# Attention stage of a two-layer kernel: pools and loads that run on across images, an image that begins within its own split, separate buffers for the two halves' planes, and a product held back

## The chip, the cores and the metric

The kernel runs on one core of a Trainium2 chip. A core has a matrix engine (TensorE; PE in the profile, its weight loads PEld), a vector engine (VectorE, DVE), a scalar engine (ScalarE, ACT), GpSimd (POOL) and SyncE (SP), whose queue issues most of the DMAs here.[...] The metric is the device time of one execution in microseconds (us), lower is better.

## The reference

`x` is 4 images of 96 channels, 128x128 pixels, float32. Two layers follow each other, each added to its input after a group norm.

```python
# layer 0: a state space block on 192 inner channels
z = silu(depthwise3x3(in_w @ gn(x)));  four scans over z (rows, columns, both ways)
x = x + out_w @ layernorm_c(y0 + y1 + y2 + y3)
# layer 1
xr, x1, x2 = relu_split_norm(gn(x))            # positive part and negative part, each normed over the image
key, qry  = conv3x3(x1, aw1), conv3x3(x2, aw2) # cut into 3x3 patches
attn      = softmax(key . qry / sqrt(C*9))     # gives a 96x96x3x3 kernel of each image
y1        = norm(conv3x3(conv3x3(x1, aw3), attn))
y2        = norm(conv3x3(x2, w_conv2)) * x1
x = x + xr + w_full @ concat(y1, y2) + b_full
```

What matters here is layer 1: the softmax needs the whole image, and only then can the last convolution (with weights made from it) begin. The split norm needs two passes over the image: sums first, then the two halves.

## The kernel before

The program is written with a tile framework: the code emits instructions in an order that is their priority, a planner orders them for each engine by that priority, by dependencies and by its own cost estimates, and a tile whose slot is still held waits for its release. Pools that are closed and opened again reuse the same memory, so the first tiles of the new pool wait for the last uses of the old one.

Two streams are interleaved by `co_run(left, light, pace)`: after each step of `left` (with a cost), steps of `light` worth `pace` times this cost are emitted. `Later` holds follow-up work (evacuations, stores) for a few ticks.

For each image b the light stream holds, in this order: `norm` (`ssm_output`: the output projection of layer 0), `split` (`split_norm`), both for the image ahead, and `close` (`attn_output`: the last 1x1 convolution and residual) of the image behind. The left stream is the attention:

- Image 0 is worked by `direct_maps`: direct 3x3 convolutions in strips of 6 rows. As it goes, `lift` turns the value map `vd` into planes `vp` (4 rows a step, 32 steps, twelve DVE instructions each, L1426 to L1435). At its end stand the remaining lifts, then `taps.weights()`: softmax, nine transposes (L1696), `products_weights` on DVE (L1258 to L1264), a store to `watd`. Its last convolution is in `attention`, which loads `watd` again (`wa`).
- Images 1 to 3 are worked by `attention` wholly. Convolutions are done over planes: each row of pixels is turned into six planes (`planes_of`), so that a 3x3 convolution takes six products for four columns. Strips are 12 rows, 11 to an image. For each strip there are two maps m (0: key and value from x1, 1: query and w_conv2 from x2); each has a first `products` of 128 output rows and a second one of 64. Their results leave PSUM through ACT copies `ends` and `odd` (L1540) and DVE sums (L1554 to L1562). `PairTaps` collects key times query. After the last strip `weights()` makes `wa`, and 11 strips m=2 of the last convolution follow, from `vp` to `od`.

`split_norm`'s second pass goes through 16 pieces of 8 rows. ACT writes the scaled input to PSUM (L1219), DVE masks it into a tile `half` (L1223; one buffer for each side, `half0` and `half1`), and `planes_of` makes six planes and stores them (L1442) in `x1p` or `x2p`. For x1 that is done by two ACT multiplications into `x4` and `x2` (L1393, L1394) and ten POOL instructions (L1401 to L1406, and L1371 four times); for x2 wholly by nine DVE instructions (`at_once`, L1376 to L1383, L1371 four times). Both go through one buffer `diff`, and share the two buffers `pl`. `value_out` does the same as the x1 form for the value map, two halves of a strip, with 128 partitions and one buffer each of `x4`, `x2`, `diff`, `pl`.

`attention` opens its pools `d1` and `d2` anew for each image, loads its first two strips (`ya`, `yc`) once they are open, and flushes its `Later` at the end. Between two images the light stream is drained.

The image loop before:

```python
light = chain(*([] if b else [light]), *after)
left = imgs[b].attend(psl)
co_run(left, light, 1.0 if b else 1.5)
drain(left)
drain(light)
```

Of the kernel before, what the change touches and what calls it, by code (L numbers as in the profile page):

```python
# [9 lines left out]
F32 = mybir.dt.float32  # L10
# [58 lines left out]
def kernel(  # L69
# [992 lines left out]
    def split_norm(xnew, x1d, x2d, stats, keep, cnt, ps, side, planes, vector):  # L1062


        with ExitStack() as pools:
# [120 lines left out]
            def stored(i, m, h):  # L1186
                if planes:
                    return planes_of(
                        later, p2, h, RS, lambda pl: store_planes(nc.sync, m, i * RS, RS, pl),
                        vector=vector(i, m is x2d),  # L1190
                    )
                at = (i * RS + 1) * PW
                return lambda: nc.scalar.dma_start(m[:, at : at + RS * PW], h)

            half = [p2.tile([C, RS * PP], F32, name=f"half{j}", bufs=1) for j in range(2)] if planes else []
            for h in half:
                nc.gpsimd.memset(h.rearrange("p (a b) -> p a b", b=PB)[:, :, TN:PB], 0.0)
            for i in range(NS):
                y = ahead.pop(0)
                piece(i + 3)  # L1200
                for side_, m in ((0, x1d), (1, x2d)):
                    op = ALU.is_le if side_ else ALU.is_gt
                    if planes:
                        h = half[side_]
# [143 lines left out]
    def planes_of(later, pool, t, r, then, most=RS, vector=False, bufs=2, p=C):  # L1348
# [6 lines left out]
        def made():  # L1355
            f = pool.tile([p, most, 6 * TN + 4], F32, name="diff", bufs=1)[:, :r]
            pl = pool.tile([p, NP, most * TN], F32, name="pl", bufs=bufs)[:, :, : r * TN]
            at, out = 0, []
            for n in (2 * PB, 2 * TN, 2 * PB):
                out.append(f[:, :, at : at + n])  # L1360
                at += n
            return out, pl

        def sums(eng, mid, outer, pl):
            f1, f2 = mid[:, :, 0:TN], mid[:, :, PB : PB + TN]
            f3, f0 = outer[:, :, 0:TN], outer[:, :, TN:]
            for i, op, x, y in (
# [3 lines left out]
                op(pl[:, i].rearrange("p (h t) -> p h t", t=TN), x, y)  # L1371

        def at_once():
            (mid, outer, df), pl = made()
# [7 lines left out]
            for i, f in ((3, AA), (4, -AA)):  # L1382
                stt(  # L1383
                    pl[:, i].rearrange("p (h t) -> p h t", t=TN),
                    df[:, :, 0:TN], f, df[:, :, PB : PB + TN], ALU.mult, ALU.add,
                )
            sums(nc.vector, mid, outer, pl)
# [9 lines left out]
        def differences(x4, x2):  # L1397
            (mid, outer, df), pl = made()
            d1, d2 = df[:, :, 0:TN], df[:, :, PB : PB + TN]
            sub, add = nc.gpsimd.tensor_sub, nc.gpsimd.tensor_add  # L1400
            sub(mid, v[:, :, 2 * PB :], x4[:, :, : 2 * PB])  # L1401
            sub(outer, v[:, :, 1 : 1 + 2 * TN], x4[:, :, 2 * PB : 2 * PB + 2 * TN])
            sub(d2, v[:, :, 3 * PB : 3 * PB + TN], v[:, :, PB : PB + TN])
            sub(d1, x2[:, :, 1, 0:TN], x2[:, :, 0, 0:TN])
            for i, op in ((3, add), (4, sub)):
                op(pl[:, i].rearrange("p (h t) -> p h t", t=TN), d2, d1)  # L1406
            sums(nc.gpsimd, mid, outer, pl)
# [174 lines left out]
    class Taps:  # L1582
# [90 lines left out]
        def weights(self):  # L1673


            self.later.flush()
# [13 lines left out]
            yield from self.rest  # L1690
# [10 lines left out]
            self.wt = wt  # L1701
            self.later.flush()
# [139 lines left out]
    def attention(img, ps):  # L1842


        with (
            tc.tile_pool(name="d1", bufs=1, side="left") as p1,
            tc.tile_pool(name="d2", bufs=2, side="left") as p2,
        ):
            later = Later()
            chunks = strips_of(AR // 2)  # L1850
            chunks = [(c[0][0], sum(r for _, r in c)) for c in chunks]
            todo = [(2, c) for c in chunks]
            if not img.mapped:
                todo = [(m, c) for c in chunks for m in (0, 1)] + todo
            maps = (img.x1p, img.x2p, img.vp)
            raw, cols = {}, {}

            def load(c, k):

                if c >= len(todo):  # L1860
                    return
                m, (r0, r) = todo[c]
# [572 lines left out]
```

## Time and profile before

| | |
|---|---|
| runs | 6845.72 us median of 3 (6822.49 to 6851.2) |
| profiled execution | 6817.06 us; its span, first to last instruction, 6815.3 us |
| mean granted TensorE clock | 0.874 of full speed |
| PE busy over the span | 5528.0 us (81%) |
| DVE busy | 4821.4 us (71%) |
| ACT busy | 3807.2 us (56%) |
| POOL busy | 3411.4 us (50%) |
| image 0's last convolution | about 3755 to 3904 us |
| image 1 | about 3990 to 4942 us |
| image 2 | about 4991 to 5942 us |
| image 3 and the end | about 5990 to 6815 us |

A share of busy time is an average over stages with different limits; the change touches only what lies behind about 3300 us. The granted clock falls to half when PE stands still, so a stall also makes the first matmuls behind it slower.

### The profile page before, as it was taken

What the parts mean: (1) busy time and instruction counts of PE and PEld (TensorE: products, weight loads), DVE (VectorE), ACT (ScalarE), POOL (GpSimd) and SP (SyncE); (2) the same over time, 40 slices, a digit from 0 to 9 for tenths busy, and PEclk for the clock granted to TensorE, in tenths of its full rate; (3) what the DMA queues carried; (4) which work ended last, traced back from release to release, by engine and by line L of the source; (5) the groups of instructions that cost most, each with busy time, mean ns of one, the idle gap of its engine ahead of it and who ended that gap; (6) DMA issues with size and microseconds to landing.
All of it is one profiled execution on the core that took longest, in us unless ns stands there. A gap on an engine that the chain in (4) does not pass through costs nothing. (4 is left out here: it accounts for less than half of the span.)

```text
span 6815.3 us, 76516 instructions
## 1 busy us (share of the span) xinstructions
PE 5528.0 (81%) x23256; PEld 2349.2 (34%) x23256; DVE 4821.4 (71%) x7737; ACT 3807.2 (56%) x4751; POOL 3411.4 (50%) x2680
## 2 busy tenths in 40 slices
PE   5889978878886519999994759876889876889986
PEld 2333323322221104444332223444333444335652
DVE  3257779989896578889547844677855676987567
ACT  1257768777875476676324534654544654544552
POOL 2236759879795439889322344466024565034410
PEclk9999989989996659999996878887989877989997
DMA  7666777866766666756656755544865555865454
GB/s 168 167 163 179 199 211 201 232 168 179 217 177 171 173 199 195 218 171 183 186 158 163 210 148 158 144 126 132 231 160 160 143 132 134 223 174 148 111 147 144
DMA packets 882103, 1176.28 MB, mean 173 GB/s; under 512 B 215230, under 2 KB 740102, under 8 KB 869212
## 3 DMA queue, kind: packets, MB, share of 16 engines
q1 hardware_dynamic: 858076, 1116.43, 60.7%
q0 software_dynamic: 16208, 38.42, 2.1%
q10 hardware_dynamic: 7408, 16.53, 0.8%
q8 instruction: 187, 3.06, 0.2%
q14 instruction: 224, 1.84, 0.1%
HBM read 766.61 MB, written 334.57 MB: 162 GB/s over the span
## 5 line engine op out<-in xcount | busy, mean ns | idle before, releaser
L621 PE MATMUL bank<-y,wp 128*128 128x512 f32 (+3 forms) x3584 | 1313.3, 624 | 86.4 <-DMA y<-y 34.7
L854 POOL TENSOR_TENSOR y<-y,dl 128x1024 f32<-128x1024 f32 x384 | 1055.1, 2748 | 268.1 <-DVE dl L846 234.9
L821 POOL TENSOR_TENSOR dl<-dl,u 128x1024 f32<-128x1024 f32 x384 | 1007.2, 2623 | 219.3 <-ACT dA L797 111.7
L842 DVE TENSOR_TENSOR_SCAN dA<-dA,pBC 128x512 f32<-128x512 f32 x768 | 981.7, 1278 | 30.8
L1469 PE MATMUL two<-ya,wd 128*64 128x192 f32 (+3 forms) x2376 | 597.3, 433 | 267.1 <-DMA ya<-x1p 91.7
L735 PE MATMUL pBC<-xr,wbc 60*128 60x512 bf16 (+1 forms) x1536 | 457.2, 403 | 329.0 <-DVE dA L842 257.7
L621 PEld LDWEIGHTS bank<-y,wp 128*128 128x128 f32 (+3 forms) x3584 | 457.7, 169 | 755.2 <-issue 656.9
L2075 PE MATMUL bank<-y,wn 128*128 128x384 f32 (+5 forms) x2408 | 685.0, 509 | 39.5 <-DMA y<-x2d 18.5
L1894 ACT COPY yb<-ya 64x768 f32<-64x768 f32 (+1 forms) x660 | 538.1, 815 | 316.1 <-PE two L1469 151.9
L846 DVE TENSOR_TENSOR dl<-dA,pBC 128x512 f32<-128x512 f32 x768 | 528.8, 689 | 259.8 <-PE pBC L735 186.1
L664 ACT ACTIVATE dl<-pd,dtb 128x512 f32<-128x512 f32 x768 | 485.6, 684 | 181.5 <-PE pd L735 167.2
L1469 PE MATMUL two<-yb,wd 128*64 128x192 f32 (+3 forms) x2376 | 568.9, 415 | 0.0
L825 DVE TENSOR_TENSOR pBC<-dl,pBC 128x512 f32<-128x512 f32 x768 | 527.2, 686 | 11.7 <-POOL dl L821 10.8
L1955 POOL COPY own<-ring 32x512 f32<-32x512 f32 (+1 forms) x198 | 214.9, 1120 | 514.9 <-DVE ring L1562 463.9
L1005 PE MATMUL bank<-y,outws 96*96 96x512 f32 x512 | 446.4, 1010 | 0.7 <-ACT st L961 0.7
L1469 PEld LDWEIGHTS two<-ya,wd 128*64 128x64 f32 (+1 forms) x2376 | 266.5, 174 | 522.2 <-issue 234.7
L2075 PEld LDWEIGHTS bank<-y,wn 128*128 128x128 f32 (+3 forms) x2408 | 313.0, 170 | 358.9 <-issue 200.7
L797 ACT ACTIVATE dA<-dl,negA 128x1024 f32<-128x1024 f32 x384 | 420.3, 1142 | 2.3
L664 ACT ACT_TABLE_LOAD x245 | 314.3, 1283 | 96.2 <-PE pd L735 89.1
L735 PEld LDWEIGHTS <-wbc 60*128 60x128 bf16 (+1 forms) x1536 | 103.4, 96 | 765.2 <-issue 751.6
L1469 PEld LDWEIGHTS two<-yb,wd 128*64 128x64 f32 (+1 forms) x2376 | 295.9, 175 | 144.7 <-issue 35.3
L1469 PE MATMUL two<-ya,wa 128*96 128x384 f32 (+1 forms) x528 | 226.5, 512 | 130.9 <-DMA wa<-watd 78.9
(307 smaller groups left out, 9546.6 us busy)
## 6 DMA issues: line engine op xcount, KB each, us to landing
u<-zb SPq DMA_DIRECT2D x192, 1024.0 KB
yms<-y SPq DMA_DIRECT2D x96, 512.0 KB
y<-yms SPq DMA_DIRECT2D x64, 768.0 KB
xn<-xnew SPq DMA_DIRECT2D x128, 384.0 KB
ya<-vp SPq DMA_DIRECT2D x120, 336.0 KB
y<-y SPq DMA_DIRECT2D x128, 258.2 KB
zb<-z SPq DMA_DIRECT2D x64, 512.0 KB
ya<-x1p SPq DMA_DIRECT2D x90, 336.0 KB
```

What stands on the lines that cost most here:

```text
L621: nc.tensor.matmul(blocks(pz[p:e]), lhsT=ws[k][:, d, c : c + e - p], rhs=window(ys[k], at, d, n), start=(i == 0), stop=(i == len(terms) - 1),)
L664: nc.scalar.activation(dst, src, AF.Softplus, bias=bias)
L735: nc.tensor.matmul(p, lhsT=w[rows], rhs=xr[rows, at : at + CH], start=True, stop=True)
L821: nc.gpsimd.tensor_mul(t, t, u_view(n))
L825: nc.vector.tensor_mul(p, live[n]["dl"][:, bass.ts(half, CH)], p)
L842: nc.vector.tensor_tensor_scan(h, h, p, init, ALU.mult, ALU.add)
L846: nc.vector.tensor_mul(live[n]["dl"][:, sl], live[n]["dA"][:, sl], live[n]["C", half])
L854: nc.gpsimd.tensor_add(v, v, t.rearrange("p (a b) -> p a b", b=W))
L1005: nc.tensor.matmul(to, lhsT=outws[:, j], rhs=rhs, start=(j == 0), stop=(j == 1))
L1469: nc.tensor.matmul(of(to[p:e], r), lhsT=w[:, i, c : c + e - p], rhs=tiles(t[k][PAIR[i]][:, SLOT[i]], o, r), start=(k == 0), stop=False,)
L1894: nc.scalar.copy(yb[k][64 * h - 64 : 64 * h, :, :n], ya[k][0:64, :, h * TN : h * TN + n])
L2075: nc.tensor.matmul(pc[p:e, :n].rearrange("p (h w) -> p h w", w=W), lhsT=w[:, c : c + e - p], rhs=v[:, :, 0:W], start=(i == 0), stop=(i == ...
```

## The change

What it does, part by part:

1. Attention's pools `d1` and `d2`, its `Later` and its list of strips become one object `Attention` for all images. The list runs on from image to image, so the first two strips of an image are loaded two strips before the image ahead of it ends. `later` is no longer flushed at an image's end; `close` ticks it until that image's last result is stored (`finished`).
2. `drain(light)` after each image goes; only ahead of images 2 and 3 is the light stream drained. So image 1 begins while its own split is still under way; a load calls `until`, which emits as many steps of the split as its rows need.
3. In `split_norm` `half0` has two buffers, the DVE form has its own planes `plv` and `diff`, and the POOL form has `pl` (one buffer) and works in place: the differences overwrite `x4` and `x2`, one goes through plane 4. The number of instructions is the same.
4. The last second product of map 1 is held back: a third of it goes ahead of the last key times query sums, two steps behind the softmax, the rest behind the making of `wa`. In `direct_maps` the held product goes ahead of those sums.
5. In `direct_maps` the remaining lifts go behind `weights()` and the store of `watd`; the pool `lifts` moves into its pools.

The core of the diff:

```diff
 def split_norm(..., done):
+                    def then(pl):
+                        store_planes(nc.sync, m, i * RS, RS, pl)
+                        done[m is x2d] = (i + 1) * RS
-            half = [p2.tile([C, RS * PP], F32, name=f"half{j}", bufs=1) for j in range(2)] if planes else []
+            half = [
+                [p2.tile([C, RS * PP], F32, name=f"half{j}{k}", bufs=1) for k in range(2 - j)]
+                for j in range(2)
...
-                        h = half[side_]
+                        h = half[side_][i % len(half[side_])]
 def planes_of(...):
         def at_once():
-            (mid, outer, df), pl = made()
+            f = pool.tile([p, most, 6 * TN + 4], F32, name="diff", bufs=1)[:, :r]
+            mid, outer, df = f[:, :, : 2 * PB], f[:, :, 2 * PB : 130], f[:, :, 130:]
+            pl, to = planes("plv", 1)
...
         def differences(x4, x2):
-            (mid, outer, df), pl = made()
-            d1, d2 = df[:, :, 0:TN], df[:, :, PB : PB + TN]
+            mid, outer = x4[:, :, : 2 * PB], x4[:, :, 2 * PB : 2 * PB + 2 * TN]
+            d1 = x2[:, :, 0, 0:TN]
+            pl, to = planes("pl", 1)
-            sub(mid, v[:, :, 2 * PB :], x4[:, :, : 2 * PB])
-            sub(outer, v[:, :, 1 : 1 + 2 * TN], x4[:, :, 2 * PB : 2 * PB + 2 * TN])
-            sub(d2, v[:, :, 3 * PB : 3 * PB + TN], v[:, :, PB : PB + TN])
-            sub(d1, x2[:, :, 1, 0:TN], x2[:, :, 0, 0:TN])
+            sub(mid, v[:, :, 2 * PB :], mid)
+            sub(outer, v[:, :, 1 : 1 + 2 * TN], outer)
+            sub(to[4], v[:, :, 3 * PB : 3 * PB + TN], v[:, :, PB : PB + TN])
+            sub(d1, x2[:, :, 1, 0:TN], d1)
+            add(to[3], to[4], d1)
+            sub(to[4], to[4], d1)
 class Taps: def weights(self):
+            rest = iter(self.rest)
+            self.later.flush()
+            for _ in range(3):
+                yield next(rest, 0.0)
             self.later.flush()
             while self.todo:
...
-            yield from self.rest
+            for _ in range(2):
+                yield next(rest, 0.0)
...
             self.wt = wt
+            yield from rest
+class Attention:                       # load, turn, strip: as in attention before, over one list
+            self.todo = [(0, 2, c) for c in self.chunks]
+            for b in range(1, NB):
+                self.todo += [(b, m, c) for c in self.chunks for m in (0, 1)]
+                self.todo += [(b, 2, c) for c in self.chunks]
+        def load(self, c, k):
...
+            if m < 2:
+                img.until(r0 + r + 2)
 def attention(img, at):
+                    rest = products(ps, jobs, pairs[m], later, evac, fill=<as before>)
+                    if m and r0 + r == H:
+                        taps.rest = rest
+                    else:
+                        yield from rest
 def direct_maps:
-            yield from lift(H)
             yield from taps.weights()
             nc.scalar.dma_start(img.watd, taps.wt)
+            yield from lift(H)
+            later.flush()
 class Image:
+        def until(self, rows):
+            while min(self.done) < min(rows, H):
+                assert next(light, 0) != 0
         def close(self, ps, side):
+            while not self.finished:
+                at.later.tick()
 the image loop:
+    at = Attention(psl, <pool d1>, <pool d2>)
+    at.begin()
...
         if b:
+            if b > 1:
+                drain(light)
...
-        light = chain(*([] if b else [light]), *after)
-        left = imgs[b].attend(psl)
+        light = chain(light, *after)
+        left = imgs[b].attend(at)
         co_run(left, light, 1.0 if b else 1.5)
         drain(left)
-        drain(light)
-        lifting.close()
+    drain(light)
     drain(imgs[NB - 1].close(psr, "right"))
```

## The prediction, made before the change was run

> **What bounds the kernel now.** I read the busy shares by stage first (the stage table cut at the places where PE stops), then the list of waits, then DVE's timeline where PE stands still. The change touches only what lies behind 3675 us. Columns of the table: stage, length, then busy us of PE, PEld, DVE, ACT, POOL, granted clock, DMA share, GB/s.
>
> ```profile
> 3675.80:3754.70 78.90, 0.05 (x1) 0.00 (x0) 66.36 (x217) 21.55 (x28) 28.37 (x60) 0.50 0.63 169
> 3754.70:3904.10 149.40, 124.30 (x396) 51.01 (x396) 118.36 (x202) 96.48 (x126) 52.40 (x70) 0.91 0.79 217
> 3904.10:3989.80 85.70, 0.09 (x3) 0.08 (x1) 50.09 (x99) 23.16 (x31) 46.01 (x63) 0.52 0.44 124
> 3989.80:4340.00 350.20, 342.96 (x1526) 137.81 (x1526) 173.65 (x343) 157.91 (x210) 138.47 (x168) 0.91 0.59 154
> 4340.00:4760.00 420.00, 303.08 (x2000) 197.62 (x2000) 305.72 (x592) 248.01 (x353) 254.23 (x338) 0.80 0.51 133
> ...
> 4779.80:4942.00 162.20, 151.92 (x472) 61.14 (x472) 134.69 (x180) 86.22 (x98) 0.00 (x0) 0.99 0.88 236
> 4942.00:4990.60 48.60, 29.63 (x56) 9.89 (x52) 35.98 (x48) 14.80 (x16) 1.53 (x3) 0.60 0.51 147
> ```
>
> Two holes stand out, 78.9 and 85.7 us without a matmul, at half clock. In the first DVE is busy for 66.4 of 78.9 us: it works off the lifts, and the weights' DVE instructions stand among them. In the second no engine is full. The beside-norm stage (3989 to 4340) is PE-bound; beside the split's second pass (4340 to 4760) PE idles 117 us with no engine over 73%.
>
> ```profile
> PE two L1469 <- DMA ya<-x1p: 91.7, 2, 85.6
> PE two L1469 <- DMA wa<-watd: 80.6, 2, 78.9
> ACT bank L1219 <- DVE half L1223: 216.9, 67, 12.0
> DVE diff L1376 <- POOL pl L1371: 132.0, 35, 7.2
> ACT x L1393 <- POOL diff L1402: 76.6, 26, 4.5
> ```
>
> These are total wait, count, longest. The first two lines are the holes. The next two are a chain: DVE's planes wait for POOL's (one `diff`), behind DVE stand the masks L1223, ACT waits for those with PSUM full, and behind ACT's L1219 stand the copies `odd` that free PE's PSUM. The last line matters below. The chain alone, in the second hole:
>
> ```profile
> 3954.01 0.70 DVE L1376 SCALAR_TENSOR_TENSOR diff<-half 96x528 f32<-96x528 f32 x1 [3.25 <-POOL pl L1371]
> ...
> 3960.92 1.40 DVE L1223 SCALAR_TENSOR_TENSOR half<-xn,kept,bank 96x512 f32<-96x512 f32 x2 [1.65 <-POOL diff L1403]
> 3965.58 0.70 DVE L1376 SCALAR_TENSOR_TENSOR diff<-half 96x528 f32<-96x528 f32 x1 [3.25 <-POOL pl L1371]
> ```
>
> A piece takes 11.6 us (3954.0 to 3965.6) for 7.2 us of DVE and 8 us of POOL work.
>
> **The change part by part**, against the profiled execution's own 6817.1 us (span 6815.3 and 1.8 around it); the median of the runs is 1.0042 times that.
>
> *Lifts behind the weights.* The last softmax scaling was at 3673.4, the last weight instruction on DVE at 3745. With the lifts out of the way the weights' DVE work (three copies of 0.45, ten operations of about 0.45) would end near 3690; store, reload and first matmul took 9.3 us (3745.4 to 3754.7); the held product now ahead of the sums costs up to 5 us of PE (its halves at 3653 and 3665). PE restarts near 3702 instead of 3755. But the twelve lifts left at 3675 (3.3 us each, 40 us of DVE) are not gone, and the strips need DVE for their sums. From 3675.8 to 3904.1 DVE has 66.4 + 118.4 = 184.7 us of work in 228.3. Were it 92% busy, as in its fuller stretches, that takes 201 us: gain 28 us, not 53. Rows for the first strips are there (20 of 32 lifts stored by 3675). ACT's `wa` loads wait as before for `watd`'s landing.
>
> *Image 1 begins within its split.* The 85.7 us go. The six pieces that were done in them (six L1376 between 3904 and 3990) now run beside image 1's strips, and a piece beside strips costs PE 117/16 = 7.3 us of idling: 44 us back. Gain 42. The loads through `until` add no instruction, only order: two pieces' stores go ahead of them on SP, and were issued by 3729. Image 1's light stream is now late by six pieces, so its `close` (of image 0) falls out of the stage 4780 to 4942 and comes beside image 2. Its price: image 3's eleven strips m=2 take 106.1 us alone, image 1's with `close` 162.2 + 48.6 = 210.8, so 105. Beside image 3's first strips: 226 us held three strips (c2d stores at 6072, 6157, 6219) of the 40.5 us that the later ones take, so again about 105. What replaces it beside m=2 is six pieces: DVE 68.5 for the strips and 6 x 7.2 = 112 us, at 92% 121 us. So 121 + 105 = 226 for 211, less 44 that the six pieces no longer cost at 4340 to 4760: gain 29. Cover: this holds only if image 2's strips start within the tail.
>
> *Loads across images.* PE waited 6.1 us for image 2's first `ya` loads, issued from 4983.6, right behind the last `od` store for which the closed pool was held; image 3's chain holds 23 us of such loads (5993.6 to 6016.7). These go; in the tail of image 2 PE idles 17 of 48 us. Gain 10 and 20.
>
> *Separate buffers, in place.* Beside the splits of images 2 and 3 (two stages of 420 us) DVE waits for POOL 48.7 us at L1376 and 28.7 at L1223 in the first, 50.4 and 25.5 in the second. Most of this goes: about 75 us each. Against it stands a price. The nine DVE instructions of a piece take 4.6 us where POOL rests (image 1: 0.70, 0.68, 0.70, twice 0.417, four times 0.417), on average 6.2 beside image 2, and 8.0 in the stretch 4606.2 to 4613.8 where POOL works throughout. The Trainium skill, "SBUF — State Buffer", "Who interferes with whom", says that a DVE instruction with two SBUF inputs and a GpSimd instruction that reads SBUF exclude each other for a whole instruction. That speaks against the change, which lets them overlap: each of nine instructions behind one POOL instruction of 0.6 to 1.1 us makes about 11.6 us a piece by the rule (estimate), 5.4 more than now, 86 us an image: the whole gain gone. By the trace's worst stretch it is 1.8 more, 28 us an image. I take the trace: 75 - 28 = 47 us of DVE an image, of which some two thirds reach PE: 30 each for images 2 and 3, and 10 for image 1's six. By the rule it would be 0, and the total 70 later.
>
> *What waits longer.* POOL's planes have one buffer, so L1406 waits for its store to land; that wait now is 5.5 us at a time (65.7 us in 12). Behind it on POOL stand the value map's copies L1955 and planes; POOL is 61% busy here. Between 0 and 48 x 5.5: I take 0 for PE. For the value map `x4` is held until POOL's last sum instead of its second subtraction: about 4.7 us more (L1404 0.64, L1406 twice 0.76, L1371 four times 0.63), and ACT's next L1393 waits for it with `ends` and `odd` behind it. Between nothing (three ticks lie between the halves) and 66 x 4.7 = 310 us; the last line of the waits shown has 26 of 2.9 us, after which PE hardly waits at all, so I take a loss of 20. `own` is zeroed by POOL (1.43 us) only when the last `od` store of the image ahead, now unflushed, has landed: 0 to 10 us an image, taken as 5 in all.
>
> *The product held back.* It is small: its matmuls stand from 6532.2 to 6535.7. Two thirds leave the path to the softmax: 2 us an image, 6 in all. The 7.8 to 10.5 us for `wa` stay.
>
> Sum: -28 - 42 - 29 - 30 - 70 + 25 - 6 = -180. 6817.1 - 180 = 6637, times 1.0042 = 6665.
>
> **The rivals.**
>
> *The gains come back at the ends.* `drain(light)` ahead of image 2 puts all of `close` at a higher priority than image 2's strips; if PE then waits, the hole is only moved to about 4950, with 150 us of `close` alone (image 3's end: 149.6) for 48.6. For it: the end of image 3 shows PE at 64% in that work. Against: in 5990 to 6216 both streams share the engines. Then the m=2 stage and `close` take 121 + 150 for 211, and image 1's part is -28 - 42 - 44 + 60 = -54; with half of the buffers' gain (-35), -20, +25 and -6, -90 is left: 6727, 6755 in the median's terms.
>
> *Everything overlaps.* Both holes go but for 10 us each of cold clock and half of the split's idling: -69 - 76, half of twice 117 and of image 1's 44 (-139), and the other gains (-65): about -350, 6467, 6494 in the median's terms. Against it: DVE's 81% over the first 228 us.
>
> *ACT is held by POOL.* The in-place value planes: 66 halves, three images, each holding ACT with `odd` behind it. At 4.7 us each that reach PE: 310 us, against 200 of gain without this item: 6927, 6956 in the median's terms. It decides from 200/66 = 3.0 us a half. For it: ACT runs in order, and two of its stalls of 4 us at L1393 (4550.7, 4611.4) stand ahead of PE's gaps of 7.0 and 9.4 us. Against: the planner can put `odd` first.
>
> *It does not do what it says.* Images 2 and 3 still start behind a drained light stream, so only image 1 gets the overlap; that is in the sum.
>
> **How the numbers follow.** My forecast 0.60 (6590 to 6750 by its own bounds, +75 and -85), the ends 0.21, everything 0.10, ACT held 0.09. A measurement of this kernel can tell about 0.5%, 34 us: 6811 to 6880 is no change. The forecast lies under it; of the ends 0.05 reach into it. So faster 0.86, same 0.06, slower 0.08. The range 6540 to 6820 takes in the forecast, most of the ends' case and the upper part of everything.
>
> **What would show it.** In the changed profile: the wait for `wa<-watd` near 25 us instead of 78.9, with attention's first matmul about 50 us earlier; no wait of tens of us for `ya<-x1p`; L1376's line no longer waiting for POOL, its mean up from 0.98 towards 1.2 us; the stage beside the split shorter by some 30 us; POOL's planes waiting for stores. Wrong if DVE's instructions lengthen by as much as its waits shrink, if a hole stands at image 2's start, or if ACT's multiplications `x<-own` wait over 150 us for POOL.

## The result, and the profile after

The changed kernel takes 6761.26 us (median of 4 runs, 6750.34 to 6777.05) against 6846.27 for the kernel before beside it (4 runs): ratio 0.9884 [0.9852, 0.9916]. A second measurement (e13 below) gave 0.9871 [0.9849, 0.9893]. That is 79 to 88 us faster. The forecast was 181 us: the direction was right, the size less than half of it. The time lies in the stated range (6540 to 6820), but outside the bounds of the forecast itself (6590 to 6750). The profiled execution took 6750.34 us, its span 6748.6, which is 67 us less than the span before. Stages below are read from one profiled execution of each kernel.

The stage table of the changed kernel, cut at the landmarks of the work: hole, image 0's strips m=2, the way to image 1's first c2d store, its strips beside the norm, its strips beside the split, its weights, its m=2 strips, the way to image 2's first c2d store, and the same beside norm and split for image 2. The columns are those of the table of before.

```profile
3674.50:3761.20 86.70, 0.00 (x1) 0.03 (x1) 75.67 (x221) 22.74 (x30) 36.12 (x62) 0.50 0.61 162
3761.20:3931.00 169.80, 142.34 (x458) 59.28 (x460) 142.90 (x238) 113.33 (x149) 70.53 (x85) 0.90 0.79 213
3931.00:3980.00 49.00, 36.81 (x222) 21.70 (x220) 44.10 (x78) 25.39 (x36) 36.30 (x46) 0.84 0.57 148
3980.00:4195.00 215.00, 190.10 (x953) 86.65 (x949) 119.23 (x204) 92.33 (x123) 101.56 (x130) 0.87 0.52 138
4195.00:4681.00 486.00, 411.75 (x2272) 222.81 (x2272) 335.97 (x630) 265.93 (x377) 257.98 (x328) 0.84 0.55 146
4681.00:4720.00 39.00, 25.10 (x96) 12.07 (x97) 29.15 (x62) 26.26 (x34) 19.05 (x24) 0.78 0.74 202
4720.00:4856.00 136.00, 119.77 (x488) 55.95 (x486) 110.42 (x205) 79.94 (x104) 25.44 (x35) 0.96 0.76 206
4856.00:4988.00 132.00, 107.18 (x326) 40.14 (x324) 121.89 (x135) 53.70 (x53) 26.76 (x28) 0.83 0.77 215
4988.00:5280.00 292.00, 286.61 (x1097) 102.16 (x1096) 133.55 (x245) 119.12 (x154) 116.72 (x141) 0.88 0.54 148
5280.00:5691.00 411.00, 321.30 (x2081) 209.52 (x2080) 343.58 (x634) 251.31 (x362) 271.68 (x347) 0.82 0.54 144
```

Three of these stages in the kernel before, cut at the same landmarks (the way to image 1's first c2d store, the way to image 2's, and image 2's strips beside the norm):

```profile
3923.00:4055.00 132.00, 62.70 (x288) 23.74 (x288) 61.64 (x120) 53.03 (x71) 64.77 (x88) 0.71 0.56 143
4983.00:5055.00 72.00, 63.35 (x287) 23.93 (x288) 31.70 (x58) 34.60 (x46) 28.14 (x38) 0.88 0.67 167
5055.00:5316.00 261.00, 260.99 (x1148) 102.82 (x1143) 129.96 (x246) 115.73 (x150) 109.24 (x133) 0.91 0.58 155
```

Three things are to be seen. The second hole (85.7 us before) is gone: from image 0's last store to image 1's first store there are 49 us with 12 of idling, where there were 132 with 69. The first hole is not shorter: 86.7 us for 78.9. And image 2's start has become long: 132 us for 72, and 292 for 261 to its fourth strip. Here `close` of image 0 now stands, DVE busy 121.9 of 132. A hole at that place was one of the prediction's signs of being wrong; 25 of the 132 us are without a matmul, where 9 of 72 were.

The list of waits of the changed kernel (total, count, longest):

```profile
DVE half L1228 <- POOL pl L1403: 30.6, 10, 7.2
ACT bank L1224 <- DVE half L1228: 123.4, 41, 30.0
ACT x L1393 <- POOL pl L1406: 89.6, 42, 8.7
ACT x L1392 <- POOL pl L1371: 89.4, 32, 7.3
PE two L1469 <- DMA wd<-wd: 86.7, 1, 86.7
```

DVE's planes (L1376, now L1378) no longer wait for POOL: 132 us of waiting are gone. ACT's wait for the masks fell from 216.9 to 123.4 us. ACT's two multiplications (L1392, L1393) now wait 179 us for POOL, where they waited 96. Of the 179, 136 stand at the value map's `x<-own`; over 150 there was to be a sign against the forecast, and it did not come. POOL's planes wait longer for their stores, as forecast: 216 us for 100. The last line is the first hole. DVE's planes beside image 2's split, by group (count, busy us, mean ns, idle before):

```profile
L1371 DVE TENSOR_TENSOR plv<-diff 96x256 f32<-96x256 f32 x60 | 43.0, 753 | 0.0
L1385 DVE SCALAR_TENSOR_TENSOR plv<-diff 96x256 f32<-96x256 f32 x30 | 22.9, 789 | 1.4 <-DMA x2p<-plv 1.3
L1383 DVE TENSOR_TENSOR diff<-half 96x528 f32<-96x528 f32 x15 | 16.5, 1101 | 0.0
L1379 DVE SCALAR_TENSOR_TENSOR diff<-half 96x512 f32<-96x512 f32 x15 | 16.1, 1076 | 0.0
L1378 DVE SCALAR_TENSOR_TENSOR diff<-half 96x528 f32<-96x528 f32 x16 | 14.2, 886 | 0.3
```

A piece costs DVE 0.89 + 1.08 + 1.10 + 2 x 0.79 + 4 x 0.75 = 7.7 us. The same sum before, in its stage 5316 to 5744, is 6.6 (1041, 853, 891, twice 608, four times 649 ns). The first of the nine did not get longer, as the prediction expected, but shorter (1041 to 886 ns); the eight others did. The last column shows what was bought with it: 0.3 us of waiting ahead of L1378, where there were 46.2:

```profile
L1376 DVE SCALAR_TENSOR_TENSOR diff<-half 96x528 f32<-96x528 f32 x14 | 14.6, 1041 | 46.2 <-POOL pl L1371 46.2
```

Why the first hole stays is in two queues and on POOL. On ACT:

```profile
3715.20 0.31 ACTq L2144 DMA_DIRECT2D watd<-ring  x1
...
3752.94 1.48 ACT L1224 ACTIVATE bank<-xn,kept 96x512 f32<-96x512 f32 x2 [29.98 <-DVE half L1228]
3754.04 0.31 ACTq L1335 DMA_DIRECT2D wa<-watd  x1
```

and on SP:

```profile
3750.26 0.56 SPq L1442 DMA_DIRECT2D vp<-pl  x1
3750.86 0.63 SPq L1335 DMA_DIRECT2D wd<-wd  x1
```

and POOL's first write in the pools that come after `lifts`:

```profile
3754.02 0.20 POOL L1723 MEMSET ring<- 128x24 f32 x2 [11.88 <-DMA vp<-pl]
```

The weights are stored 30 us earlier than before (3715.2 for 3745.4), as planned. But `wa` is loaded only at 3754.0, 3.8 us behind the store of the last lift (3750.26).

### The profile page after: what moved, and what is told of

The parts are those of the page before. It is cut to its first block, busy times and chain, and to the rows that moved or that the text cites. A ratio compares the mean times of both kernels' runs of the same rounds, so it can differ in the third digit from the quotient of the medians.

```text
span 6748.6 us, 76538 instructions
## 1 busy us (share of the span) xinstructions
PE 5562.2 (82%) x23256; PEld 2361.2 (35%) x23256; DVE 4895.1 (73%) x7737; ACT 3810.3 (56%) x4751; POOL 3441.7 (51%) x2683
## 5 line engine op out<-in xcount | busy, mean ns | idle before, releaser
L1005 PE MATMUL bank<-y,outws 96*96 96x512 f32 x512 | 455.2, 1025 | 1.8 <-DVE r L1012 1.1
L1469 PE MATMUL two<-ya,wa 128*96 128x384 f32 (+1 forms) x528 | 230.5, 520 | 132.9 <-DMA wd<-wd 86.7
```

The source lines that it names most:

```text
L1005: nc.tensor.matmul(to, lhsT=outws[:, j], rhs=rhs, start=(j == 0), stop=(j == 1))
L1469: nc.tensor.matmul(of(to[p:e], r), lhsT=w[:, i, c : c + e - p], rhs=tiles(t[k][PAIR[i]][:, SLOT[i]], o, r), start=(k == 0), stop=False,)
```

## A sum to read the runs by

From 3675 us to the end, the length is PE's idle time, plus its busy time. The trace's clock records know two values here, full and half. If every matmul took twice as long at half clock, the busy time would be what the matmuls take at full clock, plus half of the busy time that falls into half clock. Most of them do: a 128x384 product of the attention starts every 0.32 us at full clock and every 0.64 at half. Summed from the trace's records of PE and of the clock (us):

| kernel | length | PE idle | at full clock | lost to half clock |
|---|---|---|---|---|
| before | 3140 | 637 | 2226 | 277 |
| separate buffers alone (e10) | 3077 | 579 | 2225 | 273 |
| changed | 3074 | 543 | 2232 | 299 |
| changed again (e13) | 3061 | 530 | 2241 | 290 |
| lifts alone (e9) | 3092 | 522 | 2230 | 340 |
| closing work lighter (e11) | 3060 | 546 | 2220 | 294 |
| six lifts, not held back (e15) | 3033 | 507 | 2249 | 277 |

The change took 94 us of idling (107 in e13), and by this sum 22 of that (12 in e13) went into half clock. That is too much. One kind of matmul, the output projection of layer 0 in the light stream (L1005), takes 0.90 us at either clock (the last section shows it), so half clock costs it nothing. It stands in half clock for 23 us of PE's time before, 55 in the changed kernel, 38 in e13 and 59 in e9. Without it the last column is 266 before, 271 and 270 in the two traces of the changed kernel, 262 in e10 and 310 in e9. So the change itself lost some 5 us to half clock, and PE's busy time at full clock grew by 23. The matmuls are the same; what this growth is stays open. Some records are missing from each trace, and the ends of matmuls are modelled, so short waits between them count as busy.

## The experiments

Ratios are to the kernel before, timed beside each kernel; 0.001 is 6.8 us, and the numbers in brackets are 95% intervals.

### One part undone at a time

e1: the product is not held back.

```diff
-                    if m and r0 + r == H:
-                        taps.rest = rest
-                    else:
-                        yield from rest
+                    yield from rest
+                    yield from taps.some(1 if m else 2)
```

> The changed kernel (6761 us) with one part undone: each pair image's last product runs before the weights again. If holding it back is what took 28 and 23 us from the weights' stage of images 1 and 2 (67 to 39, 65 to 42 us), those stages go back to about 65 and the time to 6761 + 50 = 6811. If those stages shrank because image 0's closing work had left them, they stay near 40 and the time moves by the 6 us that I forecast: 6767.

Measured 6728.16 us, 0.9857 [0.984, 0.9874]. The weights' stages (last c2d to first od store) are 44 and 46 us instead of 39 and 43: holding back is worth 3 to 5 us there, about my forecast, not the 28 and 23 by which those stages had shrunk. Yet the kernel is not slower; by the medians it is 10 to 18 us faster, which no single stage explains and which is at the edge of the intervals.

e2: one buffer for `half0`; e3: as e2, and the value map's differences in a buffer of their own.

```diff
 e2
-                [p2.tile(..., name=f"half{j}{k}", bufs=1) for k in range(2 - j)]
+                [p2.tile(..., name=f"half{j}{k}", bufs=1) for k in range(1)]
 e3, besides
+            if p == 128:
+                f = pool.tile([p, most, 2 * PB + 2 * TN], F32, name="diff", bufs=1)[:, :r]
+                mid, outer = f[:, :, : 2 * PB], f[:, :, 2 * PB :]
```

> The changed kernel with one buffer instead of two for the half that POOL turns into planes. My theory: the second buffer is worth little, 0 to 10 us (6761 to 6771), since DVE's instructions get longer as its waits get shorter. The rival, that the separate buffers gave their full 70 us and the loss lies elsewhere, puts some 20 of them here: 6781.

> As the kernel with one half buffer, and the value map's first two differences in a buffer of their own instead of in place, so that ACT's x4 comes free after POOL's second subtraction. If ACT, held by the in-place planes (179 us of waits for POOL instead of 77), costs what I forecast, it is 20 us faster than the kernel with one half buffer, and up to 60 if the rival of ACT held by POOL is right in part; ACT's waits for POOL fall below 100 us. If the waits are covered, the two agree within 8 us.

Measured: e2 6763.07 us, 0.9903 [0.9884, 0.9922]; e3 6742.71, 0.9876 [0.9856, 0.9897]. The difference of e3 to e2 is 0.0027, 18 us, near the forecast (20), though the intervals overlap and the profiled executions differ by 4 us only. ACT's waits of `x<-own` and `x<-half` for POOL are 138 us in e2 and 81 in e3. The rival of ACT held by POOL, 310 us at full price, is out: 57 us of waits were worth about a third of themselves, if the 18 us hold. The second buffer of `half0` (e2 against the changed kernel) is worth 13 to 22 us by the ratios, which is the rival's 20 and not my 0 to 10; but these intervals overlap too.

e4: shared `diff`, `pl` and half buffers as before, nothing in place; all the rest as changed.

```diff
-            pl, to = planes("plv", 1)      # at_once
-            pl, to = planes("pl", 1)       # differences
+            (mid, outer, df), pl = made()  # both, as before
```

> The changed kernel with one part undone: one half buffer, and one diff and planes' buffer for DVE and POOL, nothing in place. My theory, that the separate buffers gave 20 to 35 us in all, says 6781 to 6796, with the stage beside image 2's split back from 411 to about 428 us and L1378's waits for POOL back at about 50 us. The rival, that they gave the 70 forecast and something else ate 50 of it, says 6825 or more.

Measured 6786.23 us, 0.9934 [0.9916, 0.9952]: 34 to 43 us slower than the changed kernel, at the upper end of my number or a little above, and well under the rival's 64. DVE's waits for POOL are back:

```profile
DVE diff L1381 <- POOL pl L1376: 118.2, 30, 11.7
```

Beside image 2's strips the split and weights' stages take 430 + 63 us instead of 411 + 43.

e5: image 1 begins behind its drained split.

```diff
-            if b > 1:
-                drain(light)
+            drain(light)
```

> The changed kernel with one part undone: image 1 begins behind its finished split, as before. By the stages of the two traces the overlap took 83 us from image 1's start and 69 from its split and m=2 stages, and gave 45 and 91 back in its norm stage and at image 2's start: 16 net, so 6777. The forecast (42 and 29) says 6832.

Measured 6769.74 us, 0.9901 [0.9883, 0.9919]: 12 to 20 us slower, at the edge of the intervals. The 71 us that I had forecast for this part are out. In this kernel the hole ahead of image 1 is 21.6 us of PE gap, not 85.6: from 3675 us to image 0's last store it takes 291 us where the kernel before took 248, since more of the split was worked off there.

e6: the lifts stand before the weights again.

```diff
+            yield from lift(H)
+            later.flush()
             yield from taps.weights()
             nc.scalar.dma_start(img.watd, taps.wt)
-            yield from lift(H)
-            later.flush()
```

> The changed kernel with one part undone: the last lifts before the weights, as before. My theory, that this part gained nothing (the hole at image 0's attention is 86.7 us after, 78.9 before): 6755 to 6768. The forecast said that it is worth 28: 6789.

Measured 6763.79 us, 0.9887 [0.9868, 0.9906], hole 88.5 us: the order of lifts and weights is worth nothing.

### Where the work could go instead

e7: six lifts a strip. e8: images 2 and 3 do not wait for the closing work of the image two before.

```diff
 e7
-                for _ in range(4 if rows < H else H // LR):
+                for _ in range(6 if rows < H else H // LR):
 e8
-                drain(light)
+                while not imgs[b - 2].closing:   # set by attn_output ahead of its strips
+                    next(light)
```

> The changed kernel with up to six lifts instead of four after each strip of the direct maps, so that about two instead of twelve are left at their end. My theory is that the hole of 86.7 us is the lifts' DVE work (some 40 us) however it is ordered: the hole falls to 45 to 55 us and the time to 6720 to 6730, since DVE is 45% busy in the stage that takes the lifts. The rival, that the hole is set by the weights' own chain and the reload: within 8 us of 6761.

> The changed kernel, where images 2 and 3 begin as soon as the head of image 0's (1's) closing work is emitted, so that the rest of it runs beside their first strips (three buffers for od and c2d, four for xnew). My theory, that what came back at image 2's start (60 and 31 us) is closing work in front of its strips instead of beside PE-bound ones: 30 to 60 us faster than the changed kernel, 6700 to 6730, with the way from image 1's last od store to image 2's first c2d store back to about 75 us. The rival, that the work costs the same wherever it stands: within 15 us of 6761.

Measured: e7 6736.53 us, 0.9859 [0.9837, 0.9882]; e8 6757.57, 0.9886 [0.9867, 0.9904]. e7 gained 8 to 17 us by the ratios, half or less of what I expected (31 to 41): its hole is 66 us in three pieces, not 45 to 55. e8 is the rival. The stage table of e8, at image 2's start, its fourth strip, its split, its m=2 strips, and image 3's first four strips:

```profile
4856.00:4920.00 64.00, 52.05 (x198) 22.76 (x196) 53.08 (x66) 27.80 (x31) 26.54 (x27) 0.89 0.69 189
4920.00:5190.00 270.00, 248.12 (x1066) 108.93 (x1067) 170.10 (x257) 109.93 (x136) 80.06 (x100) 0.84 0.59 154
5190.00:5677.00 487.00, 409.37 (x2257) 216.01 (x2256) 335.76 (x623) 268.26 (x378) 260.86 (x331) 0.86 0.54 145
5716.00:5842.00 126.00, 110.51 (x398) 49.92 (x398) 101.49 (x196) 71.69 (x93) 25.58 (x35) 0.91 0.78 209
5914.00:6181.00 267.00, 226.52 (x1030) 109.81 (x1030) 236.22 (x424) 114.19 (x129) 70.18 (x78) 0.89 0.67 178
```

Image 2's start is down to 64 us (132), as hoped, and its m=2 strips to 126 (181). But its split stage is 487 (411), and image 3's first strips take 267 us (195). The light work is late by one image's closing everywhere, and costs about the same wherever it stands. So the drain ahead of image 2 is not what took the gain.

e9: the last lifts ask for no pace, so that no pieces of the split are planned between them.

```diff
-                    yield 1.2
+                    yield 1.2 if rows < H else 0.0
```

> The changed kernel, where no piece of image 1's split is planned between the last lifts (they ask for no pace), so that on ACT the masks' scaling no longer stands between the weights' store and their reload as wa. If that block (29.98 us before wa's loads, behind DVE's lifts) keeps PE out of the hole, wa is loaded some 5 us behind the store and the hole of 86.7 us falls to about 50, the time by 10 to 30 us (6731 to 6751; the pieces come later). If wa's memory or another queue waits for the last lift, wa is still loaded only when that lift is done, and the hole falls by no more than the 15 us or so of DVE work of the pieces that left it, which come later: within 10 us of 6761.

Measured 6771.67 us, 0.992 [0.9903, 0.9938]: slower than the changed kernel by 25 us or more, with a hole of 75.6 us. Its two queues and POOL at the hole:

```profile
3712.43 0.31 ACTq L2144 DMA_DIRECT2D watd<-ring  x1
3740.22 1.48 ACT L1224 ACTIVATE bank<-xn,kept 96x512 f32<-96x512 f32 x2 [25.76 <-DVE half L1228]
3741.53 0.31 ACTq L1335 DMA_DIRECT2D wa<-watd  x1
```

```profile
3737.88 0.56 SPq L1442 DMA_DIRECT2D vp<-pl  x1
3738.48 0.62 SPq L1335 DMA_DIRECT2D wd<-wd  x1
```

```profile
3741.66 0.20 POOL L1723 MEMSET ring<- 128x24 f32 x2 [11.99 <-DMA vp<-pl]
```

`wa` follows the last lift's store by 3.65 us, as in the changed kernel (3.78) and in e1 (3.7), though that store came 12 us earlier. So the lifts in front of it set its time. A mask still stood ahead of it on ACT. But POOL's `ring` has no mask ahead of it; the trace puts its wait to that same store in both kernels, and it starts within 0.13 us of `wa`. So memory that the closed pool `lifts` held fits, and the mask isn't needed to explain it; no run had that memory elsewhere. Why e9 is slower is in the sum: it has 21 us less PE idling than the changed kernel, and 41 us more lost to half clock (39 without the projection), more than half of it in image 2's strips beside the norm:

```profile
4981.00:5291.00 310.00, 301.77 (x1065) 105.65 (x1066) 134.46 (x247) 117.91 (x152) 115.96 (x140) 0.81 0.53 143
```

PE is busy for 302 of 310 us there, at a granted clock of 0.81; the changed kernel had 0.88 and took 292.

### One part alone

e10: the kernel before with the separate buffers alone, the diff of part 3.

> The kernel before (6846 us) with one part of the change alone: separate buffers, in place. If the part is worth what its own undoing showed (34 us): 6812. If my 70 was right for a kernel whose light stream is drained, and the overlap has taken half of it (the stages beside the splits were 494 and 493 us before, 465 and 451 in the drained kernel): 6776 to 6785.

Measured 6744.02 us, 0.9884 [0.9867, 0.9902]: as fast as the whole change. Both holes, the strips between them, and the two split stages:

```profile
3677.00:3755.50 78.50, 0.02 (x1) 0.05 (x1) 76.20 (x214) 21.52 (x28) 36.25 (x60) 0.50 0.64 171
3755.50:3898.00 142.50, 123.65 (x396) 51.27 (x396) 130.14 (x213) 99.64 (x131) 57.55 (x73) 0.91 0.83 227
3898.00:3973.70 75.70, 0.41 (x1) 0.44 (x2) 64.13 (x90) 20.12 (x27) 53.48 (x60) 0.52 0.50 142
4302.00:4711.00 409.00, 317.69 (x2103) 206.65 (x2101) 341.30 (x636) 253.32 (x364) 267.59 (x341) 0.84 0.54 145
5268.00:5677.00 409.00, 314.07 (x2103) 204.47 (x2101) 342.70 (x636) 253.24 (x364) 268.61 (x341) 0.86 0.54 145
```

This kernel has both holes, 154 us with PE still, and is no slower than the one in which the second is filled. Each split stage is 18 to 20 us shorter than before, the weights' stage behind it 19 and 13.

e11: image 0's closing work without four of its DVE instructions a strip. e12: one of them goes to ACT and POOL in all images.

```diff
 e11
+                if img.b:
                     nc.vector.scalar_tensor_tensor(x1, xx, thr, x1, ...)   # and three others
 e12
-                nc.vector.scalar_tensor_tensor(e, xx, low[:, 0:1], e, ALU.mult, ALU.add)
+                nc.scalar.activation(xx, xx, AF.Copy, scale=low[:, 0:1])
+                nc.gpsimd.tensor_add(e, xx, e)
```

> The changed kernel, where image 0's closing work leaves out four of its DVE instructions a strip (both masks, the product with c2 and the addition to e; image 0's output is then another one): 16 times 5.3 us, 83 us of DVE. If DVE is what sets the 132 us between image 1's last od store and image 2's first c2d store (DVE busy 122 of 132), that way falls to 60 to 75 us and the time by 55 to 80 us, to 6680 to 6705. If the order of the loads or ACT or PE set it: less than 20 us.

> The changed kernel, where the last of the four SBUF additions of the closing work leaves DVE in all four images: ACT scales xx by low and POOL adds it to e. It takes 20.8 us of DVE an image away and adds as many of ACT and some 30 of POOL, which rest there (54 and 27 us busy of 132). If DVE sets these stages: 15 to 20 us an image, 6680 to 6705. If POOL's additions lengthen DVE's instructions as its planes do, half of that: 6720. If DVE is not what sets them: 6761 or more.

Measured: e11 6746.7 us, 0.9884 [0.9865, 0.9902]; e12 6777.64, 0.9933 [0.9918, 0.9947]. My theory, that DVE sets image 2's start, finds no support. In e11, image 1's m=2 strips and image 2's start:

```profile
4703.00:4928.00 225.00, 189.40 (x638) 79.08 (x638) 128.84 (x232) 113.81 (x133) 25.48 (x35) 0.92 0.80 223
4928.00:4995.00 67.00, 56.54 (x165) 17.19 (x163) 29.14 (x52) 25.01 (x32) 26.72 (x35) 0.71 0.52 138
```

DVE's total is down by 90 us (2243 to 2152), and image 2's start to 67. But the m=2 strips ahead of it take 225 us for 136: the planner has put the closing work there. Together 292 us against 268, with PE idle 46 against 41; the strips beside the norm behind them take 262 for 292. In the sum PE's idle time is unchanged, 546 for 543. So 90 us less of DVE's work gave nothing by the ratios (0 to 9 us slower than the changed kernel) and 14 us between the profiled executions. As the plan moved too, the run doesn't say what sets that stage, only that DVE's work alone doesn't set the time. e12 is 33 to 42 us slower than the changed kernel: with the additions on POOL, image 2's start takes 156 us for 132, and the last stage 156 for 143.

### Together, and both at once

e13: the changed kernel again; e14: separate buffers alone with six lifts; e15: e7 and e1 together; e16: e15 with the light stream ahead beside image 0's direct maps.

```diff
 e16, besides e7 and e1
-    co_run(left, light, 1.0)
+    co_run(left, light, 1.5)
```

> The changed kernel itself, beside the other kernels of this call. If the other five parts give nothing on top of the separate buffers: 0.987 to 0.990 of before, and the same as the separate buffers alone had (0.9884). If they give something that the calls hid: 0.983 or less.

> The kernel before with two things alone: the separate buffers, and up to six lifts after each strip of the direct maps instead of four. If the hole at image 0's attention (78.5 us with the separate buffers alone) is the lifts' DVE work: it falls to 40 to 50 us and the ratio from 0.9884 to about 0.984. If the gain of six lifts (17 us in the changed kernel) needed the overlap: 0.988.

> The changed kernel with six lifts and without the product held back, the two edits that were each some 17 us faster. If the two add up: 6761 - 35 = 6726, 0.983 of before. If one or both were within what runs of one kernel differ by: 0.986 to 0.988.

> As the kernel with six lifts and no product held back, with image 1's light stream planned at 1.5 instead of 1.0 beside image 0's direct maps. If light work is nearly free where PE sets the pace and DVE is 45% busy, image 1's split is well under way when the hole comes, its pieces cost some 7 us less each beside the strips, and it is 40 to 80 us faster than that kernel: 0.972 to 0.978. If the light stream's matmuls only move, or the lifts and the pieces now crowd the direct maps: within 15 us of that kernel.

Measured: e13 6736.09 us, 0.9871 [0.9849, 0.9893]; e14 6739.91, 0.9877 [0.9856, 0.9897]; e15 6707.25, 0.9825 [0.9805, 0.9844]; e16 6730.19, 0.986 [0.9841, 0.9879]. So the zero of the other parts stands (0.9884 without, 0.9871 and 0.9884 with them; the intervals leave room for some 20 us either way). In e14 the hole is 66 us for 78.5, also in three pieces, and the time is the one without the six lifts: with separate buffers alone they give nothing that can be seen. The two edits of e15 add up, and e15 is the fastest: 29 us under the changed kernel beside it, 121 under the kernel before. Its hole, by the list of PE's waits from 3600 to 3780, is in three pieces, 62 us together:

```profile
PE bank L1701 <- DVE sm L1692: 26.8, 1, 26.8
PE two L1469 <- DMA wa<-watd: 18.5, 1, 18.5
PE bank L2092 <- DMA y<-x2d: 16.7, 1, 16.7
```

Now the softmax waits for DVE, behind lifts and pieces. Running the light stream further ahead (e16) makes it worse.

e17: changed, with shared buffers and drained. e18: changed, drained, lifts first, nothing held back.

> The changed kernel with two parts undone: the shared buffers, and image 1 behind its finished split. The square so far, as ratios to before: both parts 0.9871 to 0.9884, overlap alone 0.9934, separate buffers alone 0.9901. If the two parts act on their own, the corner without both is 0.9934 + 0.0020 = 0.995. If they take the same idle time, either of them takes most of it, and this corner is back at 0.999 to 1.003.

> The changed kernel with three parts undone: image 1 begins behind its split, the last lifts stand before the weights, and no product is held back. What is left is separate buffers and the pools and loads that run on across images. If the loads are worth the 30 us that I forecast, it is 30 us under the kernel before with separate buffers alone: 0.984. If DVE's work is what the strips at images 2's and 3's start wait for, loads or not: 0.988 to 0.990.

Measured: e17 6801.62 us, 0.996 [0.9947, 0.9973]; e18 6756.24, 0.9896 [0.9876, 0.9915]. The square, as ratios to before:

| | shared buffers | separate buffers |
|---|---|---|
| image 1 behind its split | 0.9960 (e17) | 0.9901 (e5) |
| image 1 within its split | 0.9934 (e4) | 0.9871 and 0.9884 |

Within the square the two parts act on their own: separate buffers 40 and 34 to 43 us, the overlap 18 and 12 to 20. What does not add is outside it. The step from before to e17 (loads, lifts, held product) is 27 us; with separate buffers the same step, e10 to e5, is a loss of 12 (intervals overlap). And e18 beside e10 says that the loads across images give nothing once the buffers are separate. So what interacts is the separate buffers and the new order of pools and loads. The stages put most of it into image 1. From 3675 us to its first c2d store the kernel before takes 380 us, e17 361, e10 364, and e5, which has both, 368; and its strips beside the norm take 263 in e10 and 278 in e5. Either step alone shortens that stretch, and the second adds nothing.

## Why the prediction was right and wrong

- **Separate buffers, -70: right in the mechanism, too small in size.** Alone they give 79 us (0.9884 [0.9867, 0.9902]). e10 holds the in-place value map too, for which I had booked a loss of 20, so my number for this edit was -50. The two split and weights' stages give 37 and 33 us, where I had 30 and 30. DVE's piece rose to 7.7 us; I had taken the trace's 8.0. The Trainium skill, "SBUF — State Buffer", "Who interferes with whom", says that a DVE instruction with two SBUF inputs and a GpSimd instruction that reads SBUF contend for a shared port, under an exclusive lock. Read as a lock for whole instructions (which the page spells out for another case, DVE's two-port modes), that made 11.6 us by my estimate, and the gain nothing. Taken over only the DVE instructions beside which POOL works throughout (91 of 136 in the stage 5280 to 5691), a piece is 8.6 us, against 4.5 where POOL rests. So they do slow each other, but by less than that reading. Weighing the trace above it was right here. The whole measured gain is this one part; the other terms, -130 together, gave 0 to 9 on top of it.
- **Lifts behind the weights, -28: wrong.** The profile has +8, e6 nothing. The step that failed is "ACT's `wa` loads wait as before for `watd`'s landing". They are loaded 3.7 us behind the last lift's store in three kernels, whatever `watd` does. I had counted DVE's work and overlooked what the reload stands behind.
- **Image 1 within its split, -42, and the rebalance, -29: wrong in size.** The hole did go, by 57 us of idling. The square gives 12 to 20 us for both terms. The failed step is to count a hole in PE at its full length and the moved work at a fixed price: the pieces at 44 us, `close` at 105. PE's idling came back by 25 us between image 1's first and fourth strips, 16 at image 2's start, 5 behind it. Half clock took another 5 us by the corrected sum, and 23 us came back as PE's own busy time, which had no term in my sum and whose cause is open. Even drained, the hole is only 21.6 us long (e5), since light work then fills the strips ahead: it was never worth 85.7.
- **Loads across images, -30: wrong on top of the separate buffers.** e18 shows nothing there. The failed step is to add this gain to that of the buffers: with shared buffers the step to e17, whose other two parts (lifts, held product) gained nothing elsewhere, gives 27 us, though no run has the loads alone. Most of it lies at image 1's start (361 for 380), where I had named none. Image 2's start is 10 us shorter in e17 (62 for 72), as forecast, but its strips beside the norm are 7 us longer, and image 3's start gains 3, not 20. In the changed kernel image 3 takes 86 us to its first strip and 195 from there to its fourth, where it took 89 and 191. The waits for `ya` that I read there had other work behind them that was late next; I named none.
- **What waits longer, +25: near, as far as tested.** The in-place value map costs 18 us (e3 to e2, intervals overlapping) where I had 20; the 5 for `own` were not tested.
- **Product held back, -6: not shown.** 3 to 5 us in its stage, but the kernels without it were faster, 10 to 18 us (e1 against the changed kernel) and 23 (e15 against e7, 0.0034), each pair near the edge of its intervals.
- **The rivals.** "The gains come back at the ends" said 6755 us, and 6761 was measured. That is luck: its mechanism, the drain ahead of image 2, is not it, since e8 takes that away and gains nothing, and it had the buffers at half of their gain. Nor is it DVE alone (e11). "Everything overlaps" (6494) and "ACT is held by POOL" (6956) are far off.

## What to carry to other kernels

A hole in one engine's row is worth only what the other engines' work in it costs where it goes next; here 154 us of holes could stay in place without loss. Before summing gains, split a stretch into idling, work at full clock and time lost to half clock, give each its own term, and see which matmuls half clock really slows. Run each part alone and each part undone: the part that carried the gain showed 79 us alone, and only 34 to 43 when it was undone.

## What the runs showed of the hardware

PE ran at half clock in stretches without a gap in its records. From 4055 to 4317 us of the kernel before:

```profile
4055.00:4317.00 262.00, 262.00 (x1144) 104.27 (x1142) 129.03 (x245) 114.48 (x148) 107.71 (x130) 0.90 0.57 154
```

PE is busy for all of 262 us and the granted clock is 0.90, so by the sum above 0.1 x 262 = 26 us are lost there. Between kernels with the same matmuls this loss ran from 15 us (e10) to 57 (e9) in such a stage. The half-clock records come in steps of 3.4 us. The Trainium skill, "TensorE: Matmul & The Clock Gate", "The HAM clock gate", puts half clock down to an idle window of that length. That agrees with the holes here (0.50), but these stages show no such gap.

What goes ahead of the falls here is one kind of matmul. Layer 0's output projection of images 1 to 3 (L1005) reads a reordered view (`turned_view`) and writes one. Four of these matmuls at full clock, four at half clock, and four of image 0, which is not turned, at full clock:

```profile
4122.61 3.82 PE L1005 MATMUL bank<-y,outws 96*96 96x512 f32 x4
4127.51 3.78 PE L1005 MATMUL bank<-y,outws 96*96 96x512 f32 x4
2184.66 1.96 PE L1005 MATMUL bank<-y,outws 96*96 96x512 f32 x4
```

The granted clock was 1.00, 0.50 and 1.00 when they started. By the starts of the matmuls, a turned one takes 0.90 us at either clock; the plain one takes 0.43 at full and 0.85 at half. So the turned ones go no faster at full clock than the plain ones at half. Cut into steps of 3.4 us, the clock falls after those that they fill. L1005's share of two such steps (PE's and PEld's time in L1005, then clock, DMA share, GB/s):

```profile
4088.32:4091.73 3.41, 3.31 (x4) 0.36 (x2) 0.99 0.42 123
4091.73:4095.15 3.42, 0.00 (x0) 0.00 (x0) 0.51 0.00 0
```

From 3675 us on in the kernel before, 443 steps at full clock had PE busy for over 97%. The clock fell after 17 of them, and in each of the 17 L1005 had three quarters of the step or more. It fell after none of the 375 in which L1005 had less than half. In all 20 traces there are 315 such falls, all behind steps of which L1005 had at least half. No run took the reordered view away, so whether the view itself slows these matmuls, on the side that is read or the one that is written, and why the clock falls behind them, is not shown.
